# Feature order in an expert FFN, one load per pair of heads, and a new order of groups

## The chip, the cores and the metric

The kernel runs on one core of a Trainium2 chip. The metric is the time of one execution on the device in microseconds (us). TensorE is PE in the profile (its weight loads are PEld), VectorE is DVE, ScalarE is ACT, GpSimd is POOL. SyncE (SP) computes nothing: its queue issues most of the transfers (DMAs), which then run on the core's 16 DMA engines.

## The reference

The reference passes x, 64 sequences of 64 tokens with 128 features, through four layers. Each layer adds an attention-like branch and then an FFN branch, each scaled by the tanh of a gate:

```python
x = x + tanh(g_xattn[0]) * _L0_xattn_ref(_layernorm(x), ctx_1024, ctx_1024, ...)
x = x + tanh(g_ffn[0]) * _L0_ffn_ref(_layernorm(x), w_q, w_k, w_gate, value_experts, output_experts)
...
x = x + tanh(g_ffn[2]) * _L2_ffn_ref(_layernorm(x), gate_w, w_gate, w_up, w_down, sw_gate, sw_up, sw_down, ...)
x = x + tanh(g_xattn[3]) * _L3_xattn_ref(ctx_1024, ctx_1024, _layernorm(x), mask, Wo, bo)
x = x + tanh(g_ffn[3]) * _L3_ffn_ref(_layernorm(x), ...)
```

Two of the eight branches matter here. In layer 0's FFN each of 8 heads picks one of 8 experts for each token (`gm`), for its values and again for its output:

```python
gm = jax.nn.one_hot(sel, EXPERTS, dtype=x.dtype) * gates
values = jnp.einsum('bhne,ehdk,bnd->bhnk', gm, value_experts, x)
...
out = jnp.einsum('bhij,bhjk->bhik', attn, values)
out = jnp.einsum('bhne,ehkd,bhnk->bhnd', gm, output_experts, out)
return out.sum(axis=1)
```

In layer 2's FFN each token goes through two of 8 experts of 176 hidden features and through a shared expert of the same size. `combine` has the weight of each expert, `sg` that of the shared one:

```python
g = jnp.einsum('th,ehi->eti', x, w_gate)
u = jnp.einsum('th,ehi->eti', x, w_up)
eo = jnp.einsum('eti,eih->eth', jax.nn.silu(g) * u, w_down)
out = jnp.einsum('te,eth->th', combine, eo)
...
so = jax.nn.silu(x @ sw_gate) * (x @ sw_up) @ sw_down
out = out + sg * so
```

## The kernel before

The 4096 tokens are cut into 8 groups of 512. A unit of work is one of the eight branches for one group; `ORDER` (L2135) lists the 64 units as pairs "branch, group": 10 is layer 0's FFN (branch 1) for group 0, 52 is layer 2's FFN (branch 5) for group 2. Group g's units have to run in the order of the branches; units of different groups are independent.

`program` calls the units in this order, but no instruction is issued then: each is recorded. `Plan.order` then places every recorded operation on its engine with a model of costs: the operation's place in the recording is its rank, and an engine takes the lowest rank that is ready. The result is one fixed sequence for each engine, in which the units are interleaved. On the chip each engine runs its sequence strictly in order, and waits where an operand isn't there. `cost` (L244) gives a transfer 630 ns of SP's time and a number of bytes, and the model moves 220 bytes in a nanosecond over all transfers of the queue. Where the planner expects PE to be idle it puts matmuls of the identity as fillers (`keep_clock`; they show as L2158).

Layer 0's FFN (`l0_ffn`, unit at L1144): L1166 transposes the one-hots of all heads and experts, [64, 512]; L1174 stores them in DRAM as `ohd`, row h * 8 + e. For the values, L1236 multiplies a token tile by the experts' weights, and L1242 keeps the picked expert's; the values are turned by four DMAs (L1252, `vt`), attention makes `oT` (L1271), two heads above each other in each of four tiles. Then, for each pair of heads c and each pair of experts e, e + 1, L1282 loads the two rows of one-hots of the upper head, copied to 64 partitions, and in a second DMA those of the lower head to the other 64. The tile `pick` is [128, 2, 512] in bf16. L1289 (DVE) multiplies `oT[c]` by one of the two halves, and L1291 (PE) adds the product times the expert's output weights to `py`; that is 32 multiplications and 32 matmuls for a group, each matmul in two records. `k.behind(used[...])` makes the load of a pick wait for an earlier multiplication: the seventh before the newest at the time of recording.

Layer 2's FFN (`l2_ffn`, unit at L1896): the nine experts' 9 * 176 = 1584 features are cut into 12 chunks of 128 in a row and one of 48. `spread` stores the nine rows of weights per token in DRAM as `cwd`. For a chunk, L1906 loads `cb`: the row of an expert copied to as many partitions as the chunk has features of it, in one DMA for each expert that the chunk touches, 20 for a group. L1914 and L1915 (PE) make gate and up, L1917 and L1918 silu and product, L1919 (POOL) multiplies by `cb`, L1920 (PE) adds the chunk's part of the output. `l2_ffn_weights` loads the weights once; `wd`, the down weights, has its rows in the order of the chunks.

Of the kernel before, what the change touches and what calls it, by code (L numbers as in the profile page):

```python
# [21 lines left out]
BF16 = mybir.dt.bfloat16  # L22
# [5 lines left out]
P = 128  # L28
# [5 lines left out]
GT = 512  # L34
# [1098 lines left out]
def l0_ffn(k):  # L1133
    nc = k.nc
    H, E, DH, C = 8, 8, 64, 4
    W = k.l0f
# [7 lines left out]
    def unit(g):  # L1144
        xT = ln_T(k, g)

        pg = k.ps()
# [22 lines left out]
            )  # L1170
        ohT = k.tile([64, GT], BF16, tag="ohT")
        nc.scalar.copy(ohT, pt[:64, :])
        ohd = k.dram([64, GT], "ohd", BF16)
        nc.sync.dma_start(out=ohd, in_=ohT)  # L1174


        qT = [k.tile([P, GT], tag="qT") for _ in range(C)]
# [9 lines left out]
        for tp in range(2):  # L1187
            p = k.tile([P, 2, C, 2, S], tag="p")
# [3 lines left out]
            for tl in range(2):  # L1192
                for c in range(C):
                    n = tl * C + c
                    for par in range(2):
                        k.plan.wait(*qT, *kT)
                        rows = slice(64 * par, 64 * par + 64)
                        for b in range(2):
# [5 lines left out]
                                start=(n == 0),  # L1204
                                stop=False,
                                skip_group_check=True,
                            )
            for par in range(2):
                rows = slice(64 * par, 64 * par + 64)
                for b in range(2):  # L1210
                    nc.tensor.matmul(
                        sc[par][64 * b : 64 * b + 64], early[rows], k.hot[rows].rearrange("p n s -> p (n s)"),
                        start=False, stop=True, skip_group_check=True,
# [16 lines left out]
            for tl in range(2):  # L1230
                t = 2 * tp + tl
# [14 lines left out]
                used = [k.plan.ops[-1]]  # L1246
# [3 lines left out]
                for b in range(2):  # L1250
                    for par in range(2):
                        nc.sync.dma_start(  # L1252
                            out=vt[64 * par : 64 * par + 64, b], in_=av[64 * b : 64 * b + 64, :, par, :]
# [5 lines left out]
                for c in range(C):  # L1259
                    for b in range(2):  # L1260
                        for par in range(2):
                            rows = slice(64 * par, 64 * par + 64)
# [4 lines left out]
                                start=True,  # L1267
                                stop=True,
# [6 lines left out]
        for c in range(C):  # L1275
            for e in range(0, E, 2):

                pick = k.tile([P, 2, GT], BF16, tag="pick")
                for par in range(2):
                    r = (2 * c + par) * E + e  # L1280
                    with k.behind(used[max(len(used) - 7, 0)]):
                        nc.sync.dma_start(  # L1282
                            out=pick[64 * par : 64 * par + 64],
                            in_=ohd[r : r + 2, :].unsqueeze(0).to_broadcast([64, 2, GT]),
                        )
                for u in range(2):
                    n = c * E + e + u
                    so = k.tile([P, GT], tag="so")
                    nc.vector.tensor_tensor(so, oT[c], pick[:, u, :], ALU.mult)  # L1289
                    used.append(k.plan.ops[-1])  # L1290
                    nc.tensor.matmul(  # L1291
                        py, W["oe"][:, n * P : (n + 1) * P], so, start=(n == 0), stop=(n == C * E - 1)
                    )
# [522 lines left out]
def l2_ffn_weights(k):  # L1816
    k.l2f = {"gate": k.load("l2f_gate")}

    last = k.l2f["last"] = k.fixed("w_l2f_last", [P, 112])
    k.nc.gpsimd.memset(last, 0.0)  # L1820
    at, end = k.done
    for n, name in enumerate(("wg", "wu")):
        t = k.l2f[name] = k.fixed("w_l2f_" + name, [P, 1536])
        k.nc.scalar.dma_start(out=t, in_=k.a["l2f_" + name][:, :1536])
        k.nc.scalar.dma_start(out=last[:, 64 * n : 64 * n + 48], in_=k.a["l2f_" + name][:, 1536:])
        k.plan.after = k.plan.ops[at + (end - at) * (n + 1) // 3]
    src = k.a["l2f_wd"]
    wd = k.l2f["wd"] = k.fixed("w_l2f_wd", [P, 13, P])
    for n in range(18):
        r = 88 * n  # L1830
        while r < 88 * n + 88:
            end = min(88 * n + 88, (r // P + 1) * P)
            k.nc.sync.dma_start(
                out=wd[r % P : r % P + end - r, r // P, :], in_=src[r - 88 * n : end - 88 * n, n * P : (n + 1) * P]
            )
            r = end


def l2_ffn(k):
    nc = k.nc  # L1840
    E, I, HID = 8, 176, 9 * 176
    CH = [(c, min(P, HID - c)) for c in range(0, HID, P)]
    W = k.l2f

    gate = k.tg[:, 1, 2:3]

    def route(xT, g):

        pr = k.ps()
        for t in range(TG):  # L1850
            nc.tensor.matmul(
                pr[:, t * (E + 1) : (t + 1) * (E + 1)], xT[:, t * P : (t + 1) * P], W["gate"], start=True, stop=True
            )
        lg = pr[:, : TG * (E + 1)].rearrange("p (t e) -> p t e", e=E + 1)
        pb = k.tile([P, TG, E], tag="pb")
        m = k.tile([P, 4, TG], tag="m")
        nc.vector.tensor_reduce(m[:, 0], lg[:, :, 0:E], AX.X, ALU.max)
        nc.vector.tensor_tensor(pb, lg[:, :, 0:E], bc(m[:, 0], 2, E), ALU.subtract)
        nc.scalar.activation(pb, pb, AF.Exp)
        nc.vector.tensor_reduce(m[:, 1], pb, AX.X, ALU.add)  # L1860
        nc.vector.reciprocal(m[:, 1], m[:, 1])
        nc.vector.tensor_tensor(pb, pb, bc(m[:, 1], 2, E), ALU.mult)
        nc.vector.tensor_reduce(m[:, 2], pb, AX.X, ALU.max)
        oh1 = first_onehot(k, pb, m[:, 2], k.rank8, tag="l2oh1")
        nc.vector.scalar_tensor_tensor(pb, oh1, -2.0, pb, ALU.mult, ALU.add)
        nc.vector.tensor_reduce(m[:, 3], pb, AX.X, ALU.max)
        oh2 = first_onehot(k, pb, m[:, 3], k.rank8, tag="l2oh2")

        nc.vector.tensor_tensor(m[:, 0], m[:, 2], m[:, 3], ALU.add)
        nc.vector.reciprocal(m[:, 0], m[:, 0])  # L1870
        nc.vector.scalar_tensor_tensor(m[:, 2], m[:, 2], gate, m[:, 0], ALU.mult, ALU.mult)
        nc.vector.scalar_tensor_tensor(m[:, 3], m[:, 3], gate, m[:, 0], ALU.mult, ALU.mult)
        cw = k.tile([P, TG, E + 1], tag="cw")
        nc.vector.tensor_tensor(oh1, oh1, bc(m[:, 2], 2, E), ALU.mult)
        nc.vector.tensor_tensor(oh2, oh2, bc(m[:, 3], 2, E), ALU.mult)
        nc.vector.tensor_tensor(cw[:, :, 0:E], oh1, oh2, ALU.add)

        sg = k.tile([P, TG], tag="sg1")
        nc.scalar.activation(sg, lg[:, :, E], AF.Exp, scale=-1.0)
        nc.vector.tensor_scalar(sg, sg, 1.0, None, ALU.add)  # L1880
        nc.vector.reciprocal(sg, sg)
        nc.vector.tensor_scalar(cw[:, :, E], sg, gate, None, ALU.mult)
        return cw

    def spread(cw):

        pc = k.ps()
        for t in range(TG):
            nc.tensor.transpose(pc[: E + 1, t * P : (t + 1) * P], cw[:, t, :], k.ident)
        cT = k.tile([E + 1, GT], tag="cwT")  # L1890
        nc.scalar.copy(cT, pc[: E + 1, :])
        d = k.dram([E + 1, GT], "cwd")
        nc.sync.dma_start(out=d, in_=cT)
        return d

    def unit(g):  # L1896
        xT = ln_T(k, g)
        cwd = spread(route(xT, g))
        py = k.ps()
        for c, (c0, cn) in enumerate(CH):  # L1900
            cb = k.tile([P, GT], tag="cb")
            r = c0
            while r < c0 + cn:
                e = r // I
                end = min(c0 + cn, (e + 1) * I)
                nc.sync.dma_start(out=cb[r - c0 : end - c0, :], in_=cwd[e : e + 1, :].to_broadcast([end - r, GT]))  # L1906
                r = end
            pg = k.ps()
            if cn < P:
                pu = pg[64 : 64 + cn]  # L1910
                nc.tensor.matmul(pg[: 64 + cn], W["last"], xT, start=True, stop=True)
            else:
                pu = k.ps()
                nc.tensor.matmul(pg, W["wg"][:, c0 : c0 + cn], xT, start=True, stop=True)  # L1914
                nc.tensor.matmul(pu, W["wu"][:, c0 : c0 + cn], xT, start=True, stop=True)  # L1915
            h = k.tile([P, GT], tag="h")
            nc.scalar.activation(h[:cn], pg[:cn], AF.Silu)  # L1917
            nc.vector.tensor_tensor(h[:cn], h[:cn], pu, ALU.mult)  # L1918
            nc.gpsimd.tensor_tensor(h[:cn], h[:cn], cb[:cn], ALU.mult)  # L1919
            nc.tensor.matmul(py, W["wd"][:cn, c, :], h[:cn], start=(c == 0), stop=(c == len(CH) - 1))  # L1920
        yT = k.tile([P, TG, P], tag="yT")
        nc.scalar.copy(yT.rearrange("p t i -> p (t i)"), py)
        xg = k.x[g].rearrange("p t d -> p (t d)")
        nc.vector.tensor_tensor(xg, xg, transpose4(k, yT), ALU.add)

    return unit
# [44 lines left out]
def l3_ffn(k):  # L1971
# [163 lines left out]
ORDER = [  # L2135
    (int(n), int(g))
    for n, g in (
        "02 00 03 01 06 04 10 05 11 20 07 21 30 31 40 12 41 50 13 51 16 22 14 60 15 61 23 70 26 32 17 24 "
        "71 42 25 33 36 27 43 34 46 52 35 44 62 45 37 53 56 47 63 54 66 55 64 65 72 57 67 73 76 74 75 77"
    ).split()  # L2140
]

# [143 lines left out]
```

## Time and profile before

| | us |
|---|---|
| median of 3 runs | 1866.52 (1859.48 to 1867.57) |
| the profiled execution | 1898.05 |
| its span, first to last instruction | 1896.3 |
| mean granted TensorE clock | 0.975 of full |

The page cuts the span into 40 slices of 47.4 us and gives the busy share of each in tenths:

```profile
PE   8899999999999999999999999999899999999996
...
PEclk8899999999999999999999999999799999999999
DMA  6302231013324321031210022000140134153121
```

PE is nearly full from the third slice to the last but one, at nearly the full clock. Layer 0's FFN has its last matmuls (L1291) between 166 and 1174 us, slices 4 to 25; layer 2's FFN runs between 524 and 1782 us. The groups that take part in both, and the queue that issues the transfers:

```profile
L1289 DVE TENSOR_TENSOR b2k<-b2k,b2k 128x512 f32<-128x512 f32 x256 | 172.6, 722 | 28.1 <-PE ps L1291 16.1
...
q1 hardware_dynamic: 112541, 102.66, 19.4%
```

A group's line has the engine, the operation, what it writes and reads, its count, its busy time in us and the mean of one in ns; after the second bar stands the idle time of the engine just before it and what ended most of that. Several groups share a line name such as b2k: the names are those of the pools in which tiles live. The queue's line has its packets, its megabytes, and its share of the time of 16 DMA engines. In SP's own list of waits no line that waits for a `pick` or a `cb` to land appears above 14 us: SP waits most for POOL to make values (L1252, 169.6 us).

### The profile page before, as it was taken

The page shows a single profiled execution, that of the slowest core. Times are in us where ns is not written, and L with a number is a line of the kernel's source. Part 1 is how long each engine was busy: PE and PEld are TensorE (multiplying, and loading weights), DVE is VectorE, ACT ScalarE, POOL GpSimd, SP SyncE. Part 2 cuts the span into 40 slices and gives each one's busy share as a digit, 9 for nine tenths or more (in the row PEclk, how much of TensorE's full clock was granted, in tenths as well). Part 3 has the DMA queues.
Part 4 walks back from the last instruction along what each step waited for, and adds up shares of the span by engine and source line. Part 5 has one row for each costly group of instructions (what it writes and reads, how often), then busy time and mean ns, then how long its engine had stood idle before and what let it go on. Part 6 is the DMA issues. An engine that isn't in the chain of part 4 may idle for free.

```text
span 1896.3 us, 44773 instructions
## 1 busy us (share of the span) xinstructions
PE 1812.4 (96%) x16703; PEld 1067.3 (56%) x16703; DVE 1361.2 (72%) x3194; ACT 1106.3 (58%) x2957; POOL 1025.6 (54%) x1655
## 2 busy tenths in 40 slices
PE   8899999999999999999999999999899999999996
PEld 4555456555555454655565655574466555655675
DVE  6786887688767477667786668769558976855667
ACT  6564346745374253633458643877467776867655
POOL 7762446635352453413638354846577469466546
PEclk8899999999999999999999999999799999999999
DMA  6302231013324321031210022000140134153121
GB/s 189 115 22 74 60 100 26 2 34 110 104 76 115 96 57 62 11 94 44 77 44 13 12 58 75 24 3 1 40 114 25 32 104 120 36 135 101 32 74 45
DMA packets 122231, 121.11 MB, mean 64 GB/s; under 512 B 58378, under 2 KB 78485, under 8 KB 122013
## 3 DMA queue, kind: packets, MB, share of 16 engines
q1 hardware_dynamic: 112541, 102.66, 19.4%
q10 hardware_dynamic: 6400, 9.25, 1.6%
q0 software_dynamic: 3072, 6.33, 1.2%
q8 instruction: 132, 2.16, 0.5%
q14 instruction: 86, 0.70, 0.1%
HBM read 98.22 MB, written 8.18 MB: 56 GB/s over the span
## 4 chain that ended last, share of the span: by engine, by line
PE 71%; DVE 10%; POOL 8%; ACT 4%; DMA 3%; issue 3%; another core or an unknown queue 0%; SPq 0%; ACTq 0%; DVEq 0%; POOLq 0%
PE ps L1236 11%; PE ps L1291 9%; PE ps L840 8%; POOL b L776 5%; PE ps L1920 4%; PE ps L1914 4%; PE ps L1915 4%; PE ps L1470 3%; PE ps L1701 3%; PE ps L1349 3%; PE ps L1457 2%; PE ps L1663 2%; PE ps L1263 2%; PE ps L1386 1%; PE ps L1181 1%
## 5 line engine op out<-in xcount | busy, mean ns | idle before, releaser
L776 POOL TENSOR_TENSOR b<-b,neghalf 128x8 f32<-128x8 f32 (+1 forms) x208 | 303.6, 1460 | 17.0
L1291 PE MATMUL ps<-b2k,w_l0f_oe 128*128 128x512 f32 x512 | 234.8, 603 | 3.4 <-DVE b2k L1289 2.8
L1236 PE MATMUL ps<-w_l0f_ve,b2k 128*128 128x512 f32 x512 | 235.1, 599 | 0.5 <-DVE b4k L1105 0.2
L775 POOL TENSOR_SCALAR b<-b 128x8 f32<-128x8 f32 (+1 forms) x208 | 44.3, 213 | 318.8 <-DVE b L804 194.5
L1242 DVE COPY_PREDICATED b2k<-b1k,ps 128x512 f32<-128x512 int32 x224 | 161.7, 726 | 44.4 <-PE ps L1236 27.7
L1289 DVE TENSOR_TENSOR b2k<-b2k,b2k 128x512 f32<-128x512 f32 x256 | 172.6, 722 | 28.1 <-PE ps L1291 16.1
L1919 POOL TENSOR_TENSOR b2k<-b2k,b2k 128x512 f32<-128x512 f32 (+1 forms) x104 | 130.9, 1284 | 105.8 <-DMA b2k<-cwd 75.1
L1104 DVE TENSOR_REDUCE b<-ps 128x8 f32<-128x512 f32 x224 | 146.7, 682 | 52.9 <-PE ps L1674 14.8
L1291 PEld LDWEIGHTS ps<-b2k,w_l0f_oe 128*128 128x128 f32 x512 | 93.5, 190 | 120.8 <-issue 79.6
L1107 ACT ACTIVATE b4k<-b4k 128x64 f32<-128x64 f32 x512 | 125.8, 250 | 46.6 <-DVE b4k L1105 44.8
L1105 DVE TENSOR_TENSOR b4k<-ps,b 128x512 f32<-128x512 f32 x224 | 149.0, 680 | 3.1 <-PE ps L840 2.2
L1236 PEld LDWEIGHTS ps<-w_l0f_ve,b2k 128*128 128x128 f32 x512 | 93.1, 190 | 101.7 <-issue 83.5
L840 PE MATMUL ps<-ident,b2k 128*128 128x128 f32 x896 | 133.3, 277 | 9.3 <-DVE b2k L1360 3.4
L840 PEld LDWEIGHTS ps<-ident,b2k 128*128 128x128 f32 x896 | 102.3, 141 | 68.4 <-issue 32.1
L840 PE MATMUL ps<-ident,b4k 128*128 128x128 f32 x896 | 127.7, 278 | 7.0 <-ACT b4k L1689 2.0
L840 PEld LDWEIGHTS ps<-ident,b4k 128*128 128x128 f32 x896 | 102.3, 142 | 51.9 <-issue 28.4
L1918 DVE TENSOR_TENSOR b2k<-b2k,ps 128x512 f32<-128x512 f32 (+1 forms) x104 | 70.1, 683 | 73.5 <-ACT b2k L1917 38.3
L1360 DVE TENSOR_TENSOR b2k<-ps,b 128x512 f32<-128x512 f32 x128 | 87.5, 686 | 31.4 <-POOL b L1357 16.9
L1354 DVE TENSOR_REDUCE b<-b2k 128x8 f32<-128x512 f32 x128 | 84.8, 678 | 27.4 <-ACT b2k L1351 24.5
L1689 ACT ACTIVATE b4k<-b4k 128x512 f32<-128x512 f32 x128 | 76.3, 630 | 48.0 <-DVE b4k L1105 47.5
L1920 PE MATMUL ps<-b2k,w_l2f_wd 128*128 128x512 f32 (+1 forms) x208 | 102.2, 608 | 1.8 <-DVE b2k L1918 1.1
L1440 POOL TENSOR_TENSOR b4k<-b4k,b 128x512 f32<-128x512 f32 x64 | 67.5, 1075 | 65.6 <-DVE b L1437 54.6
(368 smaller groups left out, 4095.6 us busy)
## 6 DMA issues: line engine op xcount, KB each, us to landing
b2k<-ohd SPq DMA_DIRECT2D x256, 128.0 KB
b2k<-cwd SPq DMA_DIRECT2D x40, 256.0 KB
b2k<-in_ctxT SPq DMA_DIRECT2D x32, 256.0 KB
b2k<-b2k SPq DMA_DIRECT2D x128, 64.0 KB
b2k<-b2k SPq DMA_DIRECT2D x32, 128.0 KB
b2k<-cwd SPq DMA_DIRECT2D x16, 224.0 KB
b2k<-cwd SPq DMA_DIRECT2D x16, 192.0 KB
b2k<-cwd SPq DMA_DIRECT2D x16, 160.0 KB
```

Source lines behind the costliest of these rows:

```text
L776: k.nc.gpsimd.tensor_tensor(out, out, k.neghalf[:, :n], ALU.pow)
L840: k.nc.tensor.transpose(ps[:, t * P : (t + 1) * P], src[:, t, :], k.ident)
L1104: nc.vector.tensor_reduce(mx, src, AX.X, ALU.max)
L1105: nc.vector.tensor_tensor(out, src, bc(mx, 2, S), ALU.subtract)
L1107: nc.scalar.activation(out[:, n, :], out[:, n, :], AF.Exp, accum_out=den[n])
L1236: nc.tensor.matmul(pe, xT[:, t * P : (t + 1) * P], W["ve"][:, e * 512 : (e + 1) * 512], start=True, stop=True)
L1242: nc.vector.copy_predicated(acc, bc(ohi[:, t * H : (t + 1) * H, e], 2, DH), pe.rearrange("p (h d) -> p h d", d=DH))
L1289: nc.vector.tensor_tensor(so, oT[c], pick[:, u, :], ALU.mult)
L1291: nc.tensor.matmul(py, W["oe"][:, n * P : (n + 1) * P], so, start=(n == 0), stop=(n == C * E - 1))
L1360: nc.vector.tensor_tensor(n.rearrange("p c (r d) -> p (c r) d", r=2), ps.rearrange("p (h d) -> p h d", d=DH), bc(r, 2, DH), ALU.mult)
L1919: nc.gpsimd.tensor_tensor(h[:cn], h[:cn], cb[:cn], ALU.mult)
L1920: nc.tensor.matmul(py, W["wd"][:cn, c, :], h[:cn], start=(c == 0), stop=(c == len(CH) - 1))
```

## The change

Three things are changed.

Layer 2's FFN takes every eleventh feature into a chunk. Feature f = 11 p + c of the first 1408 (the eight experts) goes to partition p of chunk c, for c from 0 to 10. As 176 = 16 * 11, partition p then belongs to expert p // 16 in each of these chunks, so one tile `cbe` serves all eleven, and a tile `cbs` with the shared expert's row serves the last two. The gate and up weights lie in memory as before and are read with a step of 11 columns; the rows of `wd` are loaded in the new order.

Layer 0's FFN loads the one-hots of both heads of a pair in one DMA. `ohd` gets another shape over the same bytes, and the source of the load is a pattern of 2 heads, 64 copies and 1024 values.

`ORDER` is another list of the same 64 units.

```diff
-        ohd = k.dram([64, GT], "ohd", BF16)
-        nc.sync.dma_start(out=ohd, in_=ohT)
+
+        ohd = k.dram([H, E // 2, 2 * GT], "ohd", BF16)
+        nc.sync.dma_start(out=ohd.rearrange("h f (u n) -> (h f u) n", u=2), in_=ohT)
...
                 pick = k.tile([P, 2, GT], BF16, tag="pick")
-                for par in range(2):
-                    r = (2 * c + par) * E + e
-                    with k.behind(used[max(len(used) - 7, 0)]):
-                        nc.sync.dma_start(
-                            out=pick[64 * par : 64 * par + 64],
-                            in_=ohd[r : r + 2, :].unsqueeze(0).to_broadcast([64, 2, GT]),
-                        )
+                with k.behind(used[max(len(used) - 7, 0)]):
+                    nc.sync.dma_start(
+                        out=pick.rearrange("p u n -> p (u n)"),
+                        in_=ohd[2 * c : 2 * c + 2, e // 2 : e // 2 + 1, :].to_broadcast([2, 64, 2 * GT]),
+                    )
...
-        t = k.l2f[name] = k.fixed("w_l2f_" + name, [P, 1536])
+        t = k.fixed("w_l2f_" + name, [P, 1536])
         k.nc.scalar.dma_start(out=t, in_=k.a["l2f_" + name][:, :1536])
+        k.l2f[name] = [t[:, c:1408:11] for c in range(11)] + [t[:, 1408:]]
...
-    for n in range(18):
-        r = 88 * n
-        while r < 88 * n + 88:
-            end = min(88 * n + 88, (r // P + 1) * P)
-            k.nc.sync.dma_start(
-                out=wd[r % P : r % P + end - r, r // P, :], in_=src[r - 88 * n : end - 88 * n, n * P : (n + 1) * P]
-            )
-            r = end
+    for n in range(16):
+        k.nc.sync.dma_start(
+            out=wd[8 * n : 8 * n + 8, 0:11, :], in_=src[:, n * P : (n + 1) * P].rearrange("(q c) d -> q c d", c=11)
+        )
+    for p0, c, n, r0, rows in ((0, 11, 16, 0, 88), (88, 11, 17, 0, 40), (0, 12, 17, 40, 48)):
+        k.nc.sync.dma_start(out=wd[p0 : p0 + rows, c, :], in_=src[r0 : r0 + rows, n * P : (n + 1) * P])
...
+        cbe = k.tile([P, GT], tag="cbe")
+        nc.sync.dma_start(out=cbe, in_=cwd[0:E, :].unsqueeze(1).to_broadcast([E, 16, GT]))
+        cbs = k.tile([P, GT], tag="cbs")
+        nc.sync.dma_start(out=cbs, in_=cwd[E : E + 1, :].to_broadcast([P, GT]))
         py = k.ps()
         for c, (c0, cn) in enumerate(CH):
-            cb = k.tile([P, GT], tag="cb")
-            r = c0
-            while r < c0 + cn:
-                e = r // I
-                end = min(c0 + cn, (e + 1) * I)
-                nc.sync.dma_start(out=cb[r - c0 : end - c0, :], in_=cwd[e : e + 1, :].to_broadcast([end - r, GT]))
-                r = end
+            cb = cbe if c < 11 else cbs
...
-                nc.tensor.matmul(pg, W["wg"][:, c0 : c0 + cn], xT, start=True, stop=True)
-                nc.tensor.matmul(pu, W["wu"][:, c0 : c0 + cn], xT, start=True, stop=True)
+                nc.tensor.matmul(pg, W["wg"][c], xT, start=True, stop=True)
+                nc.tensor.matmul(pu, W["wu"][c], xT, start=True, stop=True)
...
-        "02 00 03 01 06 04 10 05 11 20 07 21 30 31 40 12 41 50 13 51 16 22 14 60 15 61 23 70 26 32 17 24 "
-        "71 42 25 33 36 27 43 34 46 52 35 44 62 45 37 53 56 47 63 54 66 55 64 65 72 57 67 73 76 74 75 77"
+        "01 03 00 02 11 10 04 21 05 20 31 30 06 13 41 12 07 40 51 23 14 50 22 15 61 60 33 24 71 16 32 25 "
+        "43 70 42 17 34 26 35 53 44 52 27 45 36 54 46 37 55 63 62 47 56 64 57 65 66 73 72 67 74 75 76 77"
```

## Prediction

> **What bounds the kernel now.** I read the page's engine rows first, then the chain of waits, the costliest groups, the list of DMA issues, and at last single stretches.
>
> ```profile
> span 1896.3 us, 44773 instructions
> ...
> PE 1812.4 (96%) x16703; PEld 1067.3 (56%) x16703; DVE 1361.2 (72%) x3194; ACT 1106.3 (58%) x2957; POOL 1025.6 (54%) x1655
> ...
> PE 71%; DVE 10%; POOL 8%; ACT 4%; DMA 3%; issue 3%; another core or an unknown queue 0%; SPq 0%; ACTq 0%; DVEq 0%; POOLq 0%
> ...
> L1291 PE MATMUL ps<-b2k,w_l0f_oe 128*128 128x512 f32 x512 | 234.8, 603 | 3.4 <-DVE b2k L1289 2.8
> ...
> L1919 POOL TENSOR_TENSOR b2k<-b2k,b2k 128x512 f32<-128x512 f32 (+1 forms) x104 | 130.9, 1284 | 105.8 <-DMA b2k<-cwd 75.1
> ...
> b2k<-ohd SPq DMA_DIRECT2D x256, 128.0 KB
> ```
>
> PE is the bound: it is idle for 1896.3 - 1812.4 = 84 us, and the list of groups by line adds that 66.8 us of its work are the planner's fillers (L2158). DMA has 3% of the chain, 57 us. SP's queue, which issues all that the change touches, has 0%: an issue saved there is worth nothing by itself. So the change can win little, and could lose much if it makes PE wait. The row to watch is the load of `pick` (b2k<-ohd), on which L1289 and then L1291 depend: DVE multiplies one half of a pick, PE uses it at once, and PE runs its instructions in the order written down beforehand. A late pick stops everything.
>
> **Fewer loads of the gate weights (L1906).** Twenty loads a group become two, 160 become 16. POOL's 75.1 us of waiting for them mostly go, but POOL isn't the bound. What counts is their part of the chain: in its listing I find 4.69 and 4.08 us at 615 to 624, 3.68 at 1556.6 and 3.90 at 1651.1, together 16.4 us. Taken: -16. One load per group (`cbe`) has 8 rows outermost, see below; the first L1919 may wait about 1 us more for it, 8 us at most, and POOL's slack covers that. The SP time saved, 144 issues by 0.38 us, is 55 us that nobody waited for. Ends: 0, and -57 if all DMA time left the chain.
>
> **Weights read with a step of 11.** L1914 and L1915 then load 128 columns that lie 44 bytes apart. Their rows: a weight load takes 190 ns, and the view of L1914 has 30.2 us of idle in 124 places put down to issue, 0.24 us each: a slot of 0.43 us, the pace at which the chain lists L1291 (58 records in 25.12 us), holds 0.19 of load and 0.24 of room. So a load may grow to 0.43 us and cost nothing. No weight load in this trace has a step, so I can't read the growth. A rule speaks against the edit: the Trainium skill, "SBUF — State Buffer", in the note on cachelines under the port table, says that reads are free only up to a step of four fp32 because lines are 16 bytes. By the row the sum is 0; by the rule, if each column costs a line of its own and the 190 ns become 4 x 190 = 760, it is 384 loads by 0.33 us, +126 us (an estimate). I take 0, the row, as it leaves room for more than twice the time. The load of `wd` becomes 19 DMAs instead of 29; nothing waits for it.
>
> **One load for both heads of a pair (L1282).** Now each of the two loads is 64 partitions of 2 KB; after, one load has 128 partitions, but its source is written as [2 heads, 64 copies, 1024]. The SP issues halve, 128 by 0.55 us = 70 us that nobody waits for. The question is what carries the bytes. The trace's records of single packets: a 2 KB packet takes 84 ns (median of 40,456 on this queue), and each DMA ends with one 4-byte packet per DMA engine used. The first pick, 64 rows, shows 16 of them; the store of `cwd` at 538.31, which has 9 rows, shows nine 2 KB packets and nine of 4 bytes. So the number of engines follows the rows outermost in the pattern. But both sides of that store have 9: no row has sides that differ. Here the Trainium skill, "DMA: Bandwidth & Descriptors", section "Why a DMA increments its semaphore by 16 and not by 1", decides: the number of engines is the largest up to 16 that divides the slowest dimension of both sides. For 2 and 128 that is **two engines**. Its table for kernel authors names this very form, a leading dimension under 16 in a broadcast.
>
> By the rows of now, a pick on 16 engines takes 8 x 84 ns = 0.7 us. On two it takes 64 x 84 ns = **5.4 us**, for 1.7 us of PE work (four L1291 records at that 0.43 us pace). A group has 16 picks, so 86.0 us of transfer, in series. The plan doesn't know it: `cost` prices a load by bytes alone, so the multiplications are placed for a 1.2 us transfer. Nor is there cover: `behind` lets a pick be issued only after the second multiplication of the pick four before it, so at most four are ahead. The stretch of one group as it is now, in the view by source line (count: shortest/median/longest in ns, first and last start in us), of the load:
>
> ```profile
> L1282 SPq DMA_DIRECT2D b2k<-ohd x32: 444/587/1452, 696.0 to 727.5; - x32
> ```
>
> and of the multiplications that read it:
>
> ```profile
> L1289 DVE TENSOR_TENSOR b2k<-b2k,b2k x32: 680/684/693, 704.2 to 732.2; 128x512 f32<-128x512 f32 x32
> ```
>
> From the first load to the last multiplication: 732.2 - 696.0 = 36.2 us. The same reading for the eight stretches gives 56.6, 46.6, 71.4, 40.3, 36.2, 36.1, 43.6 and 40.4, in sum 371 us. After: 0.8 us from the issue to the first packet (the store of cwd: issued 538.31, first packet 539.08), 86.0 us, and 0.9 us for the last two multiplications: 87.7 us a group, 702 us for eight. The difference, **+331 us**, goes to PE, because its order is fixed and it is full in these stretches:
>
> ```profile
> 696.00:736.00 40.00, 39.57 (x163) 18.38 (x163) 31.14 (x50) 9.26 (x21) 18.50 (x22) 1.00 0.40 119
> ...
> sum 410.00, PE 403.18 PEld 197.89 DVE 319.27 ACT 147.52 POOL 147.65; mean PE 50.40 PEld 24.74 DVE 39.91 ACT 18.44 POOL 18.46
> ```
>
> (columns: stretch, length, busy of PE, PEld, DVE, ACT and POOL, granted clock, DMA share, GB/s). The two engines carry other loads too. The DMA shares of the eight stretches, each times its length, make 157 us per engine; the picks are 256 loads x 64 packets x 84 ns / 16 engines = 86 of them, and some 16 of the stretch from 587 are the loads that the change removes. About 50 us of other traffic stay and now stand in line with the picks: **+50** (ends 0 and 71). This includes the loads of `vt` (L1252), which are issued between picks 1 and 3 and will land some 10 us late; the picks' transfers go on meanwhile, so nothing more is added.
>
> PE then works 403 of about 790 us in these stretches. The granted clock was 0.90 in the first 155 us, where PE was busy 138.6; it may fall further here. What is slowed lies beside transfers: taken 0, end +60.
>
> **A new order of groups.** No row prices it. It can't win more than PE's 84 idle us and 67 of fillers; the chain is 71% PE work that any order must do. Taken 0, ends -40 and +40. When PE is late, ACT and POOL get ahead, and some of the 84 idle us elsewhere are swallowed: a quarter, **-20** (ends 0 and -84).
>
> **The sum.** +331 + 50 - 16 - 20 = +345 us. The profiled execution took 1898.05 us (1.75 around its span) and would become 2243. It ran 31.5 above the median of 1866.52, and I put the difference on the median: **2210 us**.
>
> **Rivals.**
> 1. *The load spreads over 16 engines all the same* (the pattern reaches the queue in another form). For it: all loads of 64 rows did. Against it: the nine packets, and the rule. A queue reckoning with the trace's issue and multiplication times shows no stall up to 1.35 us a pick (8 engines) and 45 us at 2.7 us (4 engines), so it is faster from eight engines up. Then -16 remains: about 1850 us, with POOL's relief perhaps 1840. Chance 0.10.
> 2. *Two engines, but hidden*: a plan with half the SP issues starts the picks earlier or spreads the multiplications. If all eight stretches were as long as the longest now, 71.4 us, the loss is 8 x (87.7 - 71.4) = 130, less 36: 1960 us. Against it: at most four picks are ahead. Chance 0.04.
> 3. *The stepped weights are the bound, the picks aren't*: 1866 - 16 + 126 = 1976 us. Against it: the 0.24 us of room. Chance 0.03.
> 4. *Nothing to be told from no change*: 16 engines, and the new order gives back the 16 us. 1866 us, chance 0.03.
>
> **How the numbers follow.** The forecast has 0.80. By its own bounds it reaches from 1960, where rival 2 begins, to 1866 + 331 + 71 + 40 + 60 = 2368, and a little over if packets in a crowd take longer than 84 ns (at 6 us a pick the same sum is 77 us higher). I give 1970 to 2400: it holds rivals 2 and 3 in part and leaves out rivals 1 and 4. Slower is the forecast with rivals 2 and 3, 0.87; faster is most of rival 1 and a little of rival 4, 0.09; within 0.5%, about what a measurement tells from no change, 0.04.
>
> **What would show it.** DVE L1289 must wait for DMA b2k<-ohd, some 300 us in all where it now waits 4.4; a pick must post two completion packets, and consecutive picks land 5.4 us apart; the PE digits fall to about half in the slices of layer 0's FFN; waits for b2k<-cwd fall from 75 to under 15 us; L1914's weight loads stay under 0.43 us. If picks land within 1.5 us, the forecast is wrong and rival 1 holds; if weight loads take over 0.43 us and PE runs at their pace, rival 3.

## The result and the profile after

| | before | after |
|---|---|---|
| median, us | 1863.88 (1859.48 to 1867.57, 4 runs) | 2254.86 (2252.01 to 2255.72, 4 runs) |
| profiled execution, us | 1898.05 | 2254.32 |
| a second profiled execution, span | 1859.5 | |
| mean granted TensorE clock | 0.975; second 0.984 | 0.924 |

The ratio is 1.2113 [1.2083, 1.2142]: the kernel takes 391 us longer. The first profile of before was a disturbed execution, 34 us above its median, with one slice at a clock of 0.7; the second (run e8_before_again below) has neither, and is what after is compared with from here on.

From the page of after: the engine rows, the chain by engine, the three groups, the issues of `pick`, and the queue (L1290, L1288 and L1915 are L1291, L1289 and L1919 of before):

```profile
span 2252.6 us, 44174 instructions
...
PE 1915.4 (85%) x16697; PEld 1137.3 (50%) x16697; DVE 1374.9 (61%) x3194; ACT 1084.6 (48%) x2940; POOL 1020.0 (45%) x1655
...
q1 hardware_dynamic: 95499, 80.88, 11.4%
...
PE 15%; DVE 4%; ACT 3%; POOL 2%; issue 1%; DMA 0%; ACTq 0%; DVEq 0%; POOLq 0%; SPq 0%
...
L1290 PE MATMUL ps<-b2k,w_l0f_oe 128*128 128x512 f32 x512 | 312.2, 746 | 170.9 <-DVE b2k L1288 170.7
L1288 DVE TENSOR_TENSOR b2k<-b2k,b2k 128x512 f32<-128x512 f32 x256 | 167.8, 694 | 341.6 <-DMA b2k<-ohd 285.7
...
L1915 POOL TENSOR_TENSOR b2k<-b2k,b2k 128x512 f32<-128x512 f32 (+1 forms) x104 | 132.7, 1308 | 39.7 <-DMA b2k<-cwd 24.0
...
b2k<-ohd SPq DMA_DIRECT2D x128, 256.0 KB
```

PE, idle for 84 us in the first profile of before and 71 in the second, is idle for 2252.6 - 1915.4 = 337 us. The two lines in the middle point to the cause: 170.9 us of PE's idle time come just before L1290, which waits for DVE, and DVE's L1288 waits 285.7 us for the load of `pick`. The queue moves 80.88 MB instead of 102.66 in fewer packets, and yet the program is slower: it can't be the bytes. The chain's shares add up to only 25%: followed back from the end it breaks off at 1665.5 us, behind the last of the stretches in question, and so says nothing of them. Where a chain's shares don't come near 100%, look at the time of its first piece before you read them.

The slices, of 56.3 us now:

```profile
PE   8987769997686899689778996799679999999996
...
PEclk9999889998988899779876998999889999999999
DMA  5211111012121000110110101100112001101121
```

PE has seven dents, to 6 to 8 tenths, each with a dent of the clock in or just after it. They are layer 0's FFN of the eight groups, of which the first two share a dent. One group by source line, load and multiplication:

```profile
L1281 SPq DMA_DIRECT2D b2k<-ohd x16: 487/3848/5890, 1105.0 to 1174.9; - x16
...
L1288 DVE TENSOR_TENSOR b2k<-b2k,b2k x32: 624/687/784, 1131.7 to 1194.4; 128x512 f32<-128x512 f32 x32
```

From the first load to the last multiplication it takes 1194.4 - 1105.0 = 89.4 us, where a group of before had 36.2. The eight stretches take 95.3, 93.1, 100.2, 92.0, 86.5, 89.4, 90.2 and 90.6, in sum 737.3 us, against 372 in the second profile of before. The table by stretch (length, busy of PE, PEld, DVE, ACT and POOL, granted clock, DMA share, GB/s) has this row for the same one, and the sum of all eight:

```profile
1105.00:1194.40 89.40, 55.87 (x247) 23.30 (x245) 30.08 (x51) 12.77 (x34) 15.48 (x25) 0.74 0.15 53
...
sum 737.30, PE 480.17 PEld 215.40 DVE 287.70 ACT 144.53 POOL 102.42; mean PE 60.02 PEld 26.93 DVE 35.96 ACT 18.07 POOL 12.80
```

No engine is busy for more than two thirds of it, and the 16 DMA engines for 15%. A transfer on too few DMA engines would look like this: everything idles, the DMA share too, since it is a mean over all 16. DVE's timeline in the middle of the stretch (start, length, what, and the idle time before it) shows the pace:

```profile
1162.79 1.29 DVE L1288 TENSOR_TENSOR b2k<-b2k,b2k 128x512 f32<-128x512 f32 x2 [3.77 <-DMA b2k<-ohd]
1167.98 1.29 DVE L1288 TENSOR_TENSOR b2k<-b2k,b2k 128x512 f32<-128x512 f32 x2 [3.89 <-DMA b2k<-ohd]
1173.10 1.29 DVE L1288 TENSOR_TENSOR b2k<-b2k,b2k 128x512 f32<-128x512 f32 x2 [3.83 <-DMA b2k<-ohd]
```

Every 5.1 to 5.2 us two multiplications of 1.29 us, the rest waiting. In the records of packets each of these picks ends with two packets of 4 bytes, at 1162.42 and .43, 1167.55 and .56, 1172.67 and .68: two DMA engines, if each posts one. Picks follow each other by 5.12 us, which is 64 packets at 80 ns from one to the next.

The 393 us between the two profiles can be divided in two ways. By place: 365 in the eight stretches, 28 outside. By kind: PE idle +266, fillers +1, and +126 in which PE does the same work more slowly. Here an instruction's slot is the time from its start to the next start on PE, less idle time between them, and the 126 us are the difference of what is left of the span without idle time and without the fillers' slots, 1857.5 for 1731.1. Most of it is from the clock: 1731 x 0.984 / 0.924 is 1843 (an estimate).

### The profile page after: what moved, and what is told of

Its sections match the earlier page's. It is cut to its first block, busy times and chain, and to the rows that moved or that the text cites. A ratio compares the mean times of both kernels' runs of the same rounds, so it can differ in the third digit from the quotient of the medians.

```text
span 2252.6 us, 44174 instructions
## 1 busy us (share of the span) xinstructions
PE 1915.4 (85%) x16697; PEld 1137.3 (50%) x16697; DVE 1374.9 (61%) x3194; ACT 1084.6 (48%) x2940; POOL 1020.0 (45%) x1655
## 3 DMA queue, kind: packets, MB, share of 16 engines
q1 hardware_dynamic: 95499, 80.88, 11.4%
## 5 line engine op out<-in xcount | busy, mean ns | idle before, releaser
L1290 PE MATMUL ps<-b2k,w_l0f_oe 128*128 128x512 f32 x512 | 312.2, 746 | 170.9 <-DVE b2k L1288 170.7
L1288 DVE TENSOR_TENSOR b2k<-b2k,b2k 128x512 f32<-128x512 f32 x256 | 167.8, 694 | 341.6 <-DMA b2k<-ohd 285.7
L1290 PEld LDWEIGHTS ps<-b2k,w_l0f_oe 128*128 128x128 f32 x512 | 106.4, 227 | 356.1 <-DVE b2k L1288 292.3
L1915 POOL TENSOR_TENSOR b2k<-b2k,b2k 128x512 f32<-128x512 f32 (+1 forms) x104 | 132.7, 1308 | 39.7 <-DMA b2k<-cwd 24.0
L1294 ACT COPY b2k<-ps 128x512 f32<-128x512 f32 x8 | 4.6, 581 | 289.2 <-PE ps L1290 289.2
L840 PE MATMUL ps<-ident,b4k 128*128 128x128 f32 x896 | 133.2, 285 | 5.6 <-ACT b4k L1688 1.8
L1359 DVE TENSOR_TENSOR b2k<-ps,b 128x512 f32<-128x512 f32 x128 | 87.6, 686 | 45.9 <-POOL b L1356 17.8
L1264 PE MATMUL ps<-b2k,b2k 64*64 64x64 f32 x1024 | 47.6, 240 | 75.3 <-DMA b2k<-b2k 75.3
```

Source lines behind the costliest of these rows:

```text
L840: k.nc.tensor.transpose(ps[:, t * P : (t + 1) * P], src[:, t, :], k.ident)
L1290: nc.tensor.matmul(py, W["oe"][:, n * P : (n + 1) * P], so, start=(n == 0), stop=(n == C * E - 1))
L1359: nc.vector.tensor_tensor(n.rearrange("p c (r d) -> p (c r) d", r=2), ps.rearrange("p (h d) -> p h d", d=DH), bc(r, 2, DH), ALU.mult)
```

## The experiments

The theory: a pick whose source has 2 rows outermost is carried by two DMA engines and lands every 5.1 us, which makes some 350 of the 391 us; the other two parts add little. Its rivals: the stepped weights or the order cause a good part; or the loads of `vt`, stuck behind the picks in the queue, are a cost of their own; or the single load is slow for something else than its engines, such as its size or its issue. In each table the run of before is the median of those beside it on the same chip; a ratio is of all runs, with its 95% interval, and can differ a little from that of the medians.

**One part back or alone.** First the load of `pick` put back into after (e1), then each part alone in before.

```diff
-        ohd = k.dram([H, E // 2, 2 * GT], "ohd", BF16)
-        nc.sync.dma_start(out=ohd.rearrange("h f (u n) -> (h f u) n", u=2), in_=ohT)
+        ohd = k.dram([64, GT], "ohd", BF16)
+        nc.sync.dma_start(out=ohd, in_=ohT)
...
+                for par in range(2):
+                    r = (2 * c + par) * E + e
...
+                            out=pick[64 * par : 64 * par + 64],
+                            in_=ohd[r : r + 2, :].unsqueeze(0).to_broadcast([64, 2, GT]),
```

> The changed kernel with one part undone: a pick comes again in two loads of 64 partitions; the new feature order and the new order of groups stay. Theory (the merged load runs on two DMA engines): the whole loss of 391 us goes, L1288's kind of wait for DMA b2k<-ohd falls from 285.7 to under 10 us, the stretches shrink from 737 to about 370 us in sum, and the time is between 1830 and 1880 us. Rival (the stepped weights or the order of groups cost part of it): the time stays above 1900 us. Rival (the delayed vt loads are a cost of their own, caused by the order): waits of PE for b2k<-b2k stay near 75 us.

The reverse of this diff in before is e2, the lines on features and on `cbe` and `cbs` in before are e3, the two lines of `ORDER` e4.

> The kernel before with the merged load of a pick alone; old feature order, old order of groups. Theory: at least as slow as the whole change, 2230 to 2300 us, the stretches 90 us each, and each pick ends with two completion packets. Rival (it takes all three parts together, since the new order packs the stretches or the freed queue starts picks at once): under 2150 us.

> The kernel before with the new feature order of layer 2's FFN alone. Theory of the prediction: -16 us, 1845 to 1855 us; weight loads of gate and up at 0.32 us as in the changed kernel, and no matmul slower for it. Rival (weights with a step bound PE where loads and matmuls are not hidden): slower than before, 1880 us or more.

> The kernel before with the new order of groups alone. The prediction took 0 with ends of -40 and +40: 1825 to 1905 us, most likely within 10 us of the kernel before. Rival (the order was the harmful part): above 1905 us.

| run | us | before | ratio | stretches, us |
|---|---|---|---|---|
| e1, after with two loads | 1903.86 | 1862.11 | 1.0205 [1.0153, 1.0256] | 349.6 |
| e2, only the single load | 2280.31 | 1862.11 | 1.2232 [1.2166, 1.2299] | 756.6 |
| e3, only the features | 1894.05 | 1862.11 | 1.0162 [1.0118, 1.0206] | |
| e4, only the order | 1895.00 | 1862.11 | 1.0160 [1.0118, 1.0203] | |

The single load makes the loss: 351 us less without it, 418 more with it alone. In DVE's list of waits of e1 (engine, instruction, what ended the wait: us, times, longest) the wait is gone:

```profile
DVE b2k L1289 <- DMA b2k<-ohd: 3.5, 3, 3.0
```

And in e2 the chain of waits reaches back to the start, so it can say what the chain of after couldn't:

```profile
PE 49%; DMA 26%; DVE 11%; POOL 6%; ACT 4%; issue 2%; SPq 1%; ACTq 0%; DVEq 0%; POOLq 0%
DMA b2k<-ohd 18%; PE ps L1237 9%; PE ps L840 6%; DMA b2k<-b2k 5%; PE ps L1919 4%; POOL b L776 3%; PE ps L1290 3%; PE ps L1914 2%; PE ps L1913 2%; PE ps L1469 2%; PE ps L1700 2%; PE ps L1348 2%; PE ps L1264 2%; DVE b L1104 2%; PE ps L1385 2%
```

18% of 2276.2 us is 410 us of waiting for `pick` on the path itself; another 5% are loads b2k<-b2k, nearly all of `vt` (below). But e3 and e4 are not what was expected: each of the other two parts costs some 32 us, and with both and no single load (e1) it is 42. Beside the single load they cost nothing: after, which has all three parts, is 25 us faster than e2. So the parts don't add up, and the rival that names these two is right about 42 of 391 us at most. They are taken up below.

**The number of engines.** If the theory holds, the same single load must become fast by its outermost dimension alone. `ohd` is stored R times with the copies side by side, so that a pick's source has 2R rows outermost, each copied to 64 / R partitions; bytes, partitions and number of loads stay. The runs have R = 2, 4 and 8, in before.

```diff
+        ohd = k.dram([H * R, E // 2, 2 * GT], "ohd", BF16)
+        for r in range(R):
+            to = ohd.rearrange("(h r) f (u n) -> r h (f u) n", r=R, u=2)[r]
+            nc.sync.dma_start(out=to, in_=ohT)
...
+                        in_=ohd[2 * R * c : 2 * R * c + 2 * R, e // 2 : e // 2 + 1, :].to_broadcast([2 * R, 64 // R, 2 * GT]),
```

> The kernel before with the merged load of a pick alone, where ohd holds each row twice, so that the source is [4, 32, 1024] and its slowest dimension 4. Theory (the number of engines follows it): four completion packets a pick, transfers of 32 x 84 ns = 2.7 us, and, by the queue reckoning of the prediction, about 45 us over the kernel before: 1890 to 1930 us. Rival (one DMA in place of two is slow for another reason, such as all engines reading one spot of DRAM or SP's queue being held): 2200 us or more as with two engines.

> The same with ohd holding each row four times: slowest dimension 8. Theory: eight completion packets, 1.35 us a pick, no stall in the reckoning: 1850 to 1885 us, the last with 20 us for the three further stores of ohd. Rival: stays above 2000 us.

> The same with ohd holding each row eight times: slowest dimension 16. Theory: sixteen completion packets, 0.7 us a pick, 1845 to 1885 us; no slower than eight engines except by four more stores a group. Rival: stays above 2000 us.

The unchanged kernel ran beside them once more, as one of the four.

> The kernel before, unchanged, for a second profile: its first profiled execution took 1898 us, its other runs 1855 to 1870. Theory: the 32 us belong to that execution alone and a second profile takes 1855 to 1870. Rival: a profile of this kernel always costs it some 30 us, and the comparison of the two traces is to be corrected by them.

| rows outermost | run | us | ratio to before | stretches, us | DVE's idle time that ends with `pick`, us |
|---|---|---|---|---|---|
| 2 | e2 | 2280.31 | 1.2232 [1.2166, 1.2299] | 757 | 287 |
| 4 | e5 | 1957.83 | 1.0531 [1.0510, 1.0553] | 455 | 84.5 |
| 8 | e6 | 1911.93 | 1.0294 [1.0272, 1.0315] | 369 | 21.4 |
| 16 | e7 | 1887.62 | 1.0152 [1.0135, 1.0169] | 346 | 11.1 |
| (two loads) | e8 | 1859.00 | 0.9993 [0.9976, 1.0010] | 372 | 3.1 |

With four rows a pick ends with four packets of 4 bytes, and picks follow each other by 2.58 us, half of 5.12. The ranking is as expected; the times are not: e5, e6 and e7 lie 28, 27 and 3 us above the ranges expected of them. Size and issue are not the cause of the stall: e7 issues one load of 256 KB for a pick as e2 does, and its stretches are no longer than before's. Nor is it that one place in DRAM is read too often, though the copies spread the reads as well: in before each load reads its 2 KB 64 times, as in e2, and does not stall; a 2 KB packet of the queue takes 84 ns in the median of both. Even e7 is slower than before by 29 us, though hardly a wait for `pick` is left; it is one more kernel with another sequence (last part), and it stores `ohd` eight times for a group. A stretch's length is in part the plan's: where picks come in two loads, the sums are 318 (e10, e12), 350 (e1, e3) and 351 us (e4) against 372, and the time is longer all the same.

**The loads behind the picks.** PE's own list of waits in after has, next to the wait for the multiplications, one for attention's loads (L1264 is the matmul that reads `vt`):

```profile
PE ps L1290 <- DVE b2k L1288: 170.7, 78, 3.6
...
PE ps L1264 <- DMA b2k<-b2k: 75.3, 11, 12.6
```

SP's timeline says where it is from. It issues the loads of `vt` (L1253) between the picks:

```profile
1104.96 4.02 SPq L1281 DMA_DIRECT2D b2k<-ohd  x3
1109.04 8.81 SPq L1253 DMA_DIRECT2D b2k<-b2k  x3
1117.89 62.00 SPq L1281 DMA_DIRECT2D b2k<-ohd  x13
```

Three issues of `vt` take 8.81 us, though the one at 1104.28 took 0.59: they stand behind picks that the queue doesn't take. The packets fit: each of the three posts 14 of its 16 closing packets by 1119.03, and the last two only at 1123.37 to 1123.84, just behind a pick's two at 1123.14 and .15, as if two engines had been busy with picks. Is this a cost of its own? In e9 the first picks of a group may be issued only after the last copy that makes `oT`, which can only come when the loads of `vt` have landed:

```diff
+        used = [k.plan.ops[-1]]
         py = k.ps()
```

> The changed kernel, but the first picks of a group may be issued only after the last part of oT is there, so that no pick stands in front of the vt loads of its own group. Theory (the serial transfer of 16 picks on two engines sets the length; the wait for vt lies beside it): PE's wait of 75 us for b2k<-b2k goes, the waits for b2k<-ohd grow by more, since three picks no longer travel beside the attention: no gain, 2255 to 2330 us. Rival (the late vt loads are a cost of their own): 2160 to 2200 us.

It took 2285.93 us, 1.2293 [1.2249, 1.2337] of before: 31 us slower than after. From its list of waits:

```profile
DVE b2k L1289 <- DMA b2k<-ohd: 388.7, 110, 7.0
...
PE ps L1264 <- DMA b2k<-b2k: 12.9, 4, 7.5
```

The wait for `vt` is nearly gone, and the wait for `pick` has grown by more. The picks' own time is then bare: 88.8, 86.4, 88.7, 85.9, 88.4, 87.0, 88.1 and 87.1 us a stretch. While PE waited for `vt`, the two engines went on with the picks, so nothing is gained by taking that wait away in this manner: it isn't a cost that comes on top of theirs.

**The 32 us of the other two parts.** For e3 I looked at three things. The weights, by source line, in before and with the step in after:

```profile
L1914 PEld LDWEIGHTS ps<-b2k,w_l2f_wg x192: 186/190/333, 523.8 to 1770.6; 128*128 128x128 f32 x192
...
L1910 PEld LDWEIGHTS ps<-b2k,w_l2f_wg x192: 190/322/349, 659.1 to 2111.6; 128*128 128x128 f32 x192
L1910 PE MATMUL ps<-b2k,w_l2f_wg x192: 592/592/1254, 659.2 to 2112.0; 128*128 128x512 f32 x192
```

The load grows from 190 to 322 ns and the matmul stays at 592. All slots of the matmuls for gate and up together grow from 168.5 us in e8 to 174.7 in e3: 6 us, presumably where a load isn't hidden. Then the fillers, by line in e8 and in e3:

```profile
L2158 PE MATMUL ps<-ident 128*128 128x128 f32 x494 | 66.1, 285 | 1.4 <-POOL ident L859 1.4
```

```profile
L2155 PE MATMUL ps<-ident 128*128 128x128 f32 x736 | 98.5, 285 | 1.9 <-POOL ident L859 1.4 <-DVE w_l0f_oe L2094 0.4
```

32.4 us more of them, nearly all that e3 loses. Are the fillers themselves the cost, or do they stand in gaps that would be there without them? In e11 every third planned filler of e3 is left out:

```diff
-                result.append(o)
+                self.kept += 1
+                if self.kept % 3 < 2:
+                    result.append(o)
...
```

And does any other sequence cost that much? `ISSUE` is the planner's charge per instruction on an engine; another value plans the same work anew, in before (e10) and in e3 (e12):

```diff
-ISSUE = 14.0
+ISSUE = 15.0
```

> The kernel before with a constant of the planner's cost model, the issue time of a PE instruction, at 15 instead of 14 ns. No work is added, removed or resized; only the fixed sequences differ. Theory (the sequence of the kernel before is a lucky one, and any new one loses it): 1880 to 1905 us, as with the new order alone, the new feature order alone, and sixteen engines. Rival (those three cost what they do by their own work): within 0.5% of the kernel before, 1850 to 1868 us.

> The kernel before with the new feature order alone, where the planner still plans all its filler matmuls but every third is left out when the sequence is written down (it changes no other place). With the new feature order fillers are 736 records and 94.6 us, before they were 494 and 63.7 us. Theory (the fillers stand in gaps that aren't there on the chip, and their 31 us are the 32 us of loss): about 30 us less than with all of them, 1855 to 1875 us. Rival (the gaps are there, or the fillers hold the clock): 1885 us or more, with more idle time of PE or a lower clock.

> The kernel before with the new feature order alone, planned with the PE issue time at 15 instead of 14 ns, as in e10_other_plan. Theory (the 32 us of the new feature order come from the particular sequence that the planner made for it): another sequence gives another time, at least 10 us away from 1894, and most likely lower, 1860 to 1885 us. Rival (the new feature order costs 32 us by its own work, whatever the sequence): within 6 us of 1894, or of 1894 and the 11 us that this constant cost the kernel before, 1888 to 1911 us.

Idle time here is that between PE's instructions; the 6 us behind the last one count as the rest. The last four columns are of the profiled execution.

| run | us | ratio to before | PE idle | fillers' slots | the rest | clock |
|---|---|---|---|---|---|---|
| e8, before | 1859.00 | 0.9993 [0.9976, 1.0010] | 64.7 | 63.7 | 1731.1 | 0.984 |
| e3, features | 1894.05 | 1.0162 [1.0118, 1.0206] | 56.7 | 94.6 | 1739.8 | 0.984 |
| e4, order | 1895.00 | 1.0160 [1.0118, 1.0203] | 73.0 | 71.0 | 1751.2 | 0.973 |
| e11, fewer fillers | 1896.23 | 1.0200 [1.0172, 1.0228] | 78.0 | 71.8 | 1757.6 | 0.973 |
| e10, before planned anew | 1871.12 | 1.0066 [1.0044, 1.0088] | 67.3 | 65.3 | 1738.3 | 0.983 |
| e12, e3 planned anew | 1909.71 | 1.0269 [1.0246, 1.0292] | 75.5 | 80.6 | 1752.3 | 0.980 |

In e11 22.8 us of fillers less come back as 21.3 us of idle time: the gaps are real, and nothing is gained by leaving fillers out. The 17.8 us of slower work beside them belong to the profiled execution, which took 1909.05 us at a clock of 0.973; the other four had 0.975 to 0.981, and in the median e11 is 2 us above e3. A mere new plan of the same work costs 10.5 us (e10 fits neither of its two expectations exactly). With the features changed it is 32 us in the one plan and 1909.71 - 1871.12 = 39 in the other, within the range (1888 to 1911) that e12's rival gave for a cost of the features. But with the new order in both kernels the features add only 1903.86 - 1895.00 = 9 us (e1 and e4). So they were slower in each of three pairs, by an amount that depends on the sequence; how much is their own isn't shown, and why there are more gaps in PE's sequence stays open. The stepped loads explain about 6 us in the one plan and 3 in the other (the same slots are 173.0 us in e10 and 175.8 in e12). POOL's wait for `cwd` only goes from 61.2 us (e8) to 31.3 (e3) and 64.8 (e12), in these two all of it at the first use in a group: with two loads too, this waits for the store and the load before it. Weights stored in the chunks' order, which would have no step, were not tried. For the order (e4) no second plan was made. Its profile is 36 us longer than e8's: 8 of idle time, 7 of fillers, and 20 of slower work, which is what the lower clock would make of it (1731 x 0.984 / 0.973 = 1751, an estimate). Why the clock is lower stays open.

## Why the prediction was right

It forecast slower, by two engines and at 2210 us; it is slower by just this, at 2255, within the range. By its steps:

- **Two engines**, the step on which all rested and which the trace of before couldn't show: confirmed by the two closing packets and by the row of 2, 4, 8 and 16. The rule cited there from the Trainium skill, "DMA: Bandwidth & Descriptors", section "Why a DMA increments its semaphore by 16 and not by 1", holds in these runs. A pick took 5.12 us (5.4 said): a packet's record still has 84 ns, but the next one on its engine starts after 80. The wait of 300 us forecast for L1289 was 285.7.
- **The stretches**: +331 and +50 were forecast, +365 measured. The 87.7 us for a bare group agree with the mean of 87.6 in e9, in part by luck: sixteen picks of 5.12 us are 82 and not 86, and what is left, other traffic with it, is 5.7 and not 1.7.
- **The loads of `vt`** wait long, and add nothing: e9.
- **The clock** fell further, to 0.74 to 0.91 in the stretches, and the picks still set the pace there, as said: L1290 takes 746 ns instead of 603 while DVE waits for picks. The PE digits fall only to 6 to 8 and not to half; work done more slowly fills the slices better. Outside the stretches the clock is 0.967 against 0.984 in e8. For the 1423 us in which PE isn't idle there this makes 25 us (an estimate), a cost that the prediction had only within its end of +60. It can't be put down to the stall alone: e1, without it, has 0.970 there.
- **The stepped weights**: 322 ns, under the 430 that the row gave room for, and PE's pace is unchanged. That decides between the two prices weighed for it: 3 to 6 us were measured, where the row made 0 of it and the page's note, as it was applied there, 126. The load took 1.7 times the plain one, not 4 times.
- **What failed in size** are the terms outside the stretches: -16 for the gate weights' loads, 0 for the order, -20 for idle time swallowed, in sum -36. The measurement is +28. The -16 was read off the chain as four waits that would vanish; e3 removes those loads and is 32 us slower. The 0 for the order was +33 (e4), within the ends named; both together are +42 (e1). That the waits swallow idle time elsewhere is not borne out: PE's idle time outside the stretches is 55.5 us in e8, 68.7 in e2, 73.8 in e1 and 92.5 in after. The stretches were put 16 us too high and the rest 64 too low, so the errors partly cancel.
- **The wait for `cwd`** was to fall below 15 us; it is 24.0, and more in other plans.

Of the rivals, 16 engines, a hidden transfer and stepped weights as the bound are excluded by the same rows. The reckoning that the change would be faster than before from eight engines on was not tried with all three parts. For the single load alone it is not borne out: e6 and e7, which also store `ohd` four and eight times, are 53 and 29 us slower, with 21.4 and 11.1 us of DVE waiting for picks.

## What to carry to other kernels

Before you merge broadcast loads, look at the outermost dimension of the source pattern and not at the number of transfers: two rows copied to 128 partitions went over two DMA engines, and took 5.1 us for what would be 0.7 on 16 (8 packets of 84 ns each, an estimate). The closing packets tell how many engines carry a transfer: they were 2, 4, 8 and 16 for as many rows. If a pattern must have few rows outermost, storing those rows several times gives the engines back, though none of these runs was faster than the two loads. And where a planner fixed the sequence of before, count small savings in it at nothing: seven kernels with nearly the same work and little stall at the picks (at most 21 us), among them one with a mere other constant in the planner, were 10 to 53 us slower than before (e1, e3, e4, e6, e7, e10, e12).

## What the hardware showed beyond that

**SP is held by a slow transfer ahead.** The issue of a pick, 0.55 us in the median before, took 0.49 us at the shortest, 2.98 in the median and 6.35 at the longest in after. In the stretch shown the first two picks are issued at once, the third takes over 2.5 us, and later ones up to 5.9: the queue seems to take about two such picks ahead and then to hold SP for about the time of one. Whatever else SP issues in the meantime is late, as the three loads of `vt` were. With 4 engines and more the medians are 0.52 to 0.58 us again (e5 to e7).

**Weights 44 bytes apart** load in 322 ns instead of 190 for 128 columns in fp32, and the matmuls of 512 columns still start every 0.43 us in the median.
